# Two layers of graph attention in fp32: all groups' layer 0 before layer 1, and each projection as seven products of quarters in place of eight

## The chip, the cores and the metric

One core of a Trainium2 chip. The time is the device time of one execution in microseconds (us), the median of several executions.

## The reference, cut to what matters

`x` is 128 graphs of 128 nodes with 512 features, in fp32. Both layers have 8 heads of 64.

```python
# layer 0
Q, K, V = x @ W_q + b_q, x @ W_k + b_k, x @ W_v + b_v          # 512 x 512 each
scores = Q K^T / sqrt(64) + (x @ w_g[:D])[:, :, None] + (x @ w_g[D:])[:, None, :] + b_g + log(adj + 1e-9)
x = x + softmax(scores) @ V
# layer 1
q, k, v = x @ Wq.T + bq, x @ Wk.T + bk, x @ Wv.T + bv
logits = q k^T / sqrt(64) + log(clip(adj, 1e-8))
x = layer_norm(x + (softmax(logits) @ v) @ Wo.T + bo) * gamma + beta
```

Per group of four graphs these are three projections in layer 0 and four in layer 1, each a product of 512 x 512 (nodes by features) with 512 x 512 (weights). The softmax is computed without its maximum, and the log of the adjacency as a factor after `exp`.

## The kernel before

A group goes through layer 0 and, a step later, layer 1. The result of layer 0 stays in SBUF. A projection is 16 matmuls of 512 columns (V of layer 0: 32 of 256), each bank evicted by one instruction.

```python
def qk(W, bias, dst, e):
    p = ps.tile([P, G * N], F32, tag="proj", name=f"pqk_{g}_{L}_{e}")
    for c in range(KC):
        nc.tensor.matmul(p, W[L][:, c, e * P : (e + 1) * P], XT[g, L][:, :, c], start=(c == 0), stop=(c == KC - 1))
    nc.scalar.activation(dst[g, L][:, e].rearrange("p b n -> p (b n)"), p, AF.Identity, bias=bias[L][:, e : e + 1])
# ... cut: V, gate (two more columns of V's matmul in layer 0), scores, exp, multiply, second product
def part3(b):                                   # output projection, one graph
    aT = aTs[b // 2][:, b % 2]
    po = ps.tile([P, D], F32, tag="proj", name=f"po_{g}_{b}")
    for c in range(KC):
        nc.tensor.matmul(po, aT[:, c], WO[:, c], start=(c == 0), stop=(c == KC - 1))
    h = work.tile([P, D], F32, tag="h", name=f"h_{g}_{b}", bufs=3)
    nc.vector.tensor_tensor(h, po, X1[g][:, b], ALU.add)
    layer_norm(nc, small, h, GA, BE, minus_half, f"{g}_{b}")
# ... cut
for s in range(NG + 2):                         # one layer's projections beside another's attention
    a = proj_units(s, 0) if s < NG else []
    b = attn_units(s - 2, 1) if s >= 2 else []
    turned(merged(a, b), feature_units(s - 1, 1) if 1 <= s <= NG else [], 14)
    # ... cut
    a = proj_units(s - 1, 1) if 1 <= s <= NG else []
    b = attn_units(s, 0) if s < NG else []
    turned(merged(a, b), turn_units(s + 1) if s + 1 < NG else [], 14)
```

## Time and profile before

| | before |
|---|---|
| time, first three runs | 3999.66 us median (3997.59 to 4001.03) |
| span of the profiled run, mean granted TensorE clock | 3994.5 us, 0.992 |
| busy: TensorE, VectorE, GpSimd, ScalarE | 98%, 34%, 20%, 16% |
| HBM read, written | 84.16 MB, 33.55 MB |

The prediction below shows the lines. One more is used later: the granted clock in 40 equal slices of the span, in tenths of full speed (9 is 90% or more).

```profile
PEclk9999999999999999999999999999999999999988
```

It is at 90% or more until the last two slices.

### The profile page before, as it was taken

The page shows a single profiled execution, that of the slowest core. Times are in us where ns is not written, and L with a number is a line of the kernel's source. Part 1 is how long each engine was busy: PE and PEld are TensorE (multiplying, and loading weights), DVE is VectorE, ACT ScalarE, POOL GpSimd, SP SyncE. Part 2 cuts the span into 40 slices and gives each one's busy share as a digit, 9 for nine tenths or more (in the row PEclk, how much of TensorE's full clock was granted, in tenths as well). Part 3 has the DMA queues.
Part 4 walks back from the last instruction along what each step waited for, and adds up shares of the span by engine and source line. Part 5 has one row for each costly group of instructions (what it writes and reads, how often), then busy time and mean ns, then how long its engine had stood idle before and what let it go on. Part 6 is the DMA issues. An engine that isn't in the chain of part 4 may idle for free.

```text
span 3994.5 us, 41932 instructions
## 1 busy us (share of the span) xinstructions
PE 3902.6 (98%) x16386; PEld 2248.2 (56%) x16386; DVE 1376.7 (34%) x2723; ACT 636.5 (16%) x801; POOL 798.0 (20%) x839
## 2 busy tenths in 40 slices
PE   7999999999999999999999999999999999999986
PEld 4555555555555555555555555555555555555543
DVE  2233333333333333333333333333333333333332
ACT  1111111111111111111111111111111111111110
POOL 0122112122112122121221121221212211212221
PEclk9999999999999999999999999999999999999988
DMA  5212222222122122222221221222221222222111
GB/s 142 48 35 56 43 45 48 48 41 55 38 48 48 35 56 46 42 48 49 39 56 38 47 48 35 55 47 43 48 49 37 56 41 44 48 42 49 32 29 25
DMA packets 930039, 187.69 MB, mean 47 GB/s; under 512 B 892848, under 2 KB 892848, under 8 KB 929840
## 3 DMA queue, kind: packets, MB, share of 16 engines
q1 hardware_dynamic: 929840, 184.98, 22.5%
q8 instruction: 133, 2.18, 0.2%
q14 instruction: 66, 0.54, 0.0%
HBM read 84.16 MB, written 33.55 MB: 29 GB/s over the span
## 4 chain that ended last, share of the span: by engine, by line
PE 97%; SPq 1%; DVE 1%; issue 1%; POOL 0%; DMA 0%; ACT 0%; DVEq 0%; POOLq 0%
PE pqk L155 45%; PE av L249 12%; PE po L302 11%; PE pv L171 11%; PE pv L188 11%; PE s L224 7%; SPq L114 0%; SPq L86 0%; DVE t L239 0%; DMA wq<-in_L_gnn_W_q_dram 0%; POOL h L356 0%; POOL h L357 0%; DMA out_dram<-h 0%; DVE at L275 0%; DMA aT<-at 0%
## 5 line engine op out<-in xcount | busy, mean ns | idle before, releaser
L155 PE MATMUL pqk<-xT,wq 128*128 128x512 f32 x2048 | 942.5, 603 | 24.1 <-DMA wq<-in_L_gnn_W_q_dram 22.2
L155 PE MATMUL pqk<-xT,wk 128*128 128x512 f32 x2048 | 933.5, 598 | 0.0
L155 PEld LDWEIGHTS pqk<-xT,wk 128*128 128x128 f32 x2048 | 376.9, 190 | 428.1 <-issue 417.1
L155 PEld LDWEIGHTS pqk<-xT,wq 128*128 128x128 f32 x2048 | 373.1, 191 | 427.2 <-issue 410.4
L249 PEld LDWEIGHTS av<-v,t 128*128 128x128 f32 x4096 | 498.5, 194 | 130.9 <-issue 124.4
L239 DVE TENSOR_TENSOR t<-t,adjT 128x1024 f32<-128x1024 f32 x256 | 337.1, 1317 | 615.6 <-ACT t L232 615.6
L249 PE MATMUL av<-v,t 128*128 128x65 f32 x4096 | 498.3, 275 | 26.4 <-DVE at L275 24.0
L302 PE MATMUL po<-wo,aT 128*128 128x512 f32 x1024 | 466.0, 604 | 24.8 <-PE pv L171 14.0
L171 PE MATMUL pv<-wv,xT 128*128 128x256 f32 (+1 forms) x2048 | 465.3, 380 | 0.0
L188 PE MATMUL pv<-wv,xT 128*128 128x512 f32 x1024 | 453.1, 595 | 0.0
L171 PEld LDWEIGHTS pv<-wv,xT 128*128 128x128 f32 x2048 | 385.4, 189 | 93.3 <-issue 44.0
L282 POOL TENSOR_TENSOR x<-x,x 128x512 f32<-128x512 f32 x128 | 163.1, 1274 | 1096.2 <-DVE x L275 1096.2
L224 PEld LDWEIGHTS s<-qT,kT 64*128 64x128 f32 x4096 | 249.3, 188 | 191.0 <-issue 186.5
L302 PEld LDWEIGHTS po<-wo,aT 128*128 128x128 f32 x1024 | 194.9, 193 | 246.5 <-issue 205.5
L162 ACT ACTIVATE qT<-pqk,bq 128x512 f32<-128x512 f32 x256 | 175.9, 687 | 888.5 <-PE pqk L155 888.5
L188 PEld LDWEIGHTS pv<-wv,xT 128*128 128x128 f32 x1024 | 189.8, 190 | 215.2 <-issue 215.2
L162 ACT ACTIVATE kT<-pqk,bk 128x512 f32<-128x512 f32 x256 | 176.0, 688 | 798.4 <-PE pqk L155 798.4
L224 PE MATMUL s<-qT,kT 64*128 64x128 f32 x4096 | 298.4, 285 | 3.5 <-ACT t L232 3.5
L203 POOL TENSOR_TENSOR x<-x,bo 128x512 f32<-128x512 f32 x128 | 172.2, 1378 | 538.2 <-DMA xT<-x 538.2
L268 DVE TENSOR_SCALAR gated<-av,gate 128x8 f32<-128x8 f32 x128 | 28.9, 226 | 669.9 <-PE av L249 669.9
L232 ACT ACTIVATE t<-s 128x1024 f32<-128x1024 f32 x128 | 131.1, 1024 | 604.2 <-PE s L224 601.6
L176 DVE TENSOR_TENSOR v<-pv,bv 128x256 f32<-128x256 f32 x256 | 107.2, 419 | 299.4 <-PE pv L171 294.1
(39 smaller groups left out, 1578.9 us busy)
## 6 DMA issues: line engine op xcount, KB each, us to landing
x<-in_x_dram SPq DMA_DIRECT2D x32, 1024.0 KB, 5.5
xT<-in_x_dram SPq DMA_DIRECT2D x512, 64.0 KB, 2.5
xT<-x SPq DMA_DIRECT2D x512, 64.0 KB, 2.1
aT<-at SPq DMA_DIRECT2D x1024, 32.0 KB, 1.9
out_dram<-h SPq DMA_DIRECT2D x128, 256.0 KB, 2.1
adjT<-in_adj_dram SPq DMA_DIRECT2D x128, 64.0 KB, 2.3
wq<-in_L_gnn_W_q_dram SPq DMA_DIRECT2D x1, 1024.0 KB, 5.8
wk<-in_L_gnn_W_k_dram SPq DMA_DIRECT2D x1, 1024.0 KB, 8.0
```

The lines of the kernel that those rows point to most:

```text
L155: nc.tensor.matmul(p, W[L][:, c, e * P : (e + 1) * P], XT[g, L][:, :, c], start=(c == 0), stop=(c == KC - 1),)
L162: nc.scalar.activation(dst[g, L][:, e].rearrange("p b n -> p (b n)"), p, AF.Identity, bias=bias[L][:, e : e + 1])
L171: nc.tensor.matmul(p[:, 0:n], XT[g, L][:, b, c], wv0[:, c, s * W2 : s * W2 + n], start=(c == 0), stop=(c == KC - 1),)
L176: nc.vector.tensor_tensor(V[g, L][:, b, h2, 0:HD], p[:, 0:W2].rearrange("p (h d) -> p h d", d=HD), BV[L][:, s * W2 : (s + 1) * W2].rearran ...
L188: nc.tensor.matmul(p, XT[g, L][:, b, c], wv1[:, c], start=(c == 0), stop=(c == KC - 1))
L203: nc.gpsimd.tensor_tensor(X1[g][:, b], X1[g][:, b], BO, ALU.add)
L224: nc.tensor.matmul(s[:, r, c], KT[g, L][r * HD : (r + 1) * HD, c, b], QT[g, L][r * HD : (r + 1) * HD, c, b], start=True, stop=True,)
L232: nc.scalar.activation(t, s.rearrange("p r c j -> p (r c) j"), AF.Exp, scale=SCALE, **({"bias": AC[g][:, b, 1:2]} if L == 0 else {}),)
L239: nc.vector.tensor_tensor(t, t, AT2[g][:, L, b : b + 1, :].to_broadcast([P, H, N]), ALU.mult)
L249: nc.tensor.matmul(a4[:, h // KC, h % KC], t[:, (h % 2) * KC + h // 2], V[g, L][:, b, h], start=True, stop=True,)
L282: nc.gpsimd.tensor_tensor(dst, dst, X[g][:, b], ALU.add)
L302: nc.tensor.matmul(po, aT[:, c], WO[:, c], start=(c == 0), stop=(c == KC - 1))
```

## The change

Its intent is to take an eighth off the projections. The 512 x 512 operands are cut into quarters, and seven products of sums of quarters (Strassen's scheme in Winograd's form) replace the eight products. The sums of the weights are made once, which needs one layer's weights at a time in SBUF: hence layer 0 of all 32 groups first, its result to DRAM, then layer 1. The sums of X are made by GpSimd for each group. The seven products are combined by VectorE as they leave PSUM. The gate's two columns go from TensorE to VectorE, and layer 0's `b_v` is added to X for the residual by GpSimd.

```diff
+    ORDER = ("P1", "P6", "P7", "P5", "P2", "P3", "P4")
+    OPERANDS = {
+        "P1": (A11, "B11"), "P2": (A12, "B21"), "P3": (S4, "B22"), "P4": (NA22, "T4"),
+        "P5": (S1, "T1"), "P6": (S2, "T2"), "P7": (S3, "T3"),
+    }
...
+    SUMS = {"T1": ("B12", "B11"), "T2": ("B22", "T1"), "T3": ("B22", "B12"), "T4": ("T2", "B21")}
+    def sums(Bs, name, tag, which=tuple(SUMS)):
+        for s in which:
+            a, b = SUMS[s]
+            Bs[s] = act.tile([P, 2, 2, N], F32, tag=f"{tag}{s}", name=f"{s}_{name}")
+            nc.gpsimd.tensor_tensor(Bs[s], Bs[a], Bs[b], ALU.subtract)
+    def natural_units(t):
...
+            for s in range(2):                                   # the gate, in layer 0
+                junk = work.tile([P, D], F32, tag="junk", name=f"junk_{t}_{b}_{s}", bufs=1)
+                nc.vector.scalar_tensor_tensor(
+                    junk, XN[t, b // 2][:, b % 2], 1.0, WG[:, s], op0=ALU.mult, op1=ALU.mult,
+                    accum_out=C[t][:, s, b : b + 1],
+                )
+        def bias(k):
+            r = ROWS[L].rearrange("p (o d) -> p o d", o=1).to_broadcast([P, 2, D])
+            nc.gpsimd.tensor_tensor(XN[t, k], XN[t, k], r, ALU.add)
...
+        def unit(i):                                             # one product and its addition
+            if i in ("P1", "P6", "P7", "P5", "P4"):
+                t[i] = ps.tile([P, 2, D2], F32, tag="proj", name=f"p{name}_{i}", bufs=4)
+            bank = t[{"P2": "P1", "P3": "P5"}.get(i, i)]         # P2 onto P1's bank, P3 onto P5's
+            product(i, W, Bs, bank, side)
...
+            elif i == "P5":
+                o = dst(1, 1)
+                add(o, shape(bank, o), shape(t["u3b"], o))
...
+    for t in range(LAST + 1):                                    # 32 steps of layer 0, 32 of layer 1, one more
...
+        for i in range(max(len(proj), len(heads))):
+            if i < len(heads):
+                heads[i]()                                       # attention of the step before
+            if i < len(proj):
+                proj[i]()                                        # V, Q, K: 7 products each
...
+            if i >= 7 and side:
+                side.pop(0)()
+            for _ in range(2):
+                if has_out and proj and i >= 16 and turns:
+                    turns.pop(0)()                               # transposes of the attention output, then its sums
+            if i == 17 and sums_:
+                sums_.pop(0)()                                   # GpSimd's sums of the next group's X
+        for u in side + sums_:
+            u()
+        if has_out:
...
+            units, late = out_units()                            # output projection; late is layer norm
```

## The prediction

> **What bounds the kernel now.** I read the page first, then the chain of waits, then the groups by shape, then the timeline at the first group and at the end, where attention runs without projections beside it.
>
> ```profile
> PE 3902.6 (98%) x16386; PEld 2248.2 (56%) x16386; DVE 1376.7 (34%) x2723; ACT 636.5 (16%) x801; POOL 798.0 (20%) x839
> PE 97%; SPq 1%; DVE 1%; issue 1%; POOL 0%; DMA 0%; ACT 0%; DVEq 0%; POOLq 0%
> PE pqk L155 45%; PE av L249 12%; PE po L302 11%; PE pv L171 11%; PE pv L188 11%; PE s L224 7%; SPq L114 0%; SPq L86 0%; DVE t L239 0%; DMA wq<-in_L_gnn_W_q_dram 0%; POOL h L356 0%; POOL h L357 0%; DMA out_dram<-h 0%; DVE at L275 0%; DMA aT<-at 0%
> ```
>
> TensorE is the bound: 97% of the chain, 78% of it projections (45+11+11+11). The other engines are at most a third busy. The chain in order of time gives the pace of each kind:
>
> ```profile
> 1995.67 6.92 PE pv L188 x16
> 2002.59 1.73 PE av L249 x16
> 2011.24 1.09 PE s L224 x16
> 2061.59 3.47 PE pv L171 x16
> ```
>
> The profile has two records for each fp32 matmul. A record of 512 columns takes 6.92/16 = 0.4325 us, one of 256 takes 3.47/16 = 0.217, one of attention's second product (av) 1.73/16 = 0.108, one of the scores (s) 1.09/16 = 0.068. From these rows the work is 6144 x 0.4325 + 2048 x 0.217 + 4096 x 0.108 + 4096 x 0.068 = 2657 + 444 + 443 + 279 = 3823 us of 3994.5. The remainder is about 24 us at the start, about 46 at the end, and 2 to 3 us in each of 32 groups, mostly the 0.14 us by which a projection block after attention is longer.
>
> **What the Trainium skill says.**
> - TensorE: Matmul & The Clock Gate, Back-to-back issue gap: 256 columns take N/2.4 + 2.5 = 109 ns. Our records of 256 take twice that, and there are two of each matmul; I use the measured 0.217.
> - The same page, opening table: the queue pulls weight loads ahead of matmuls, and the other engines' queues are strict FIFO. So a matmul that waits holds all behind it. The trace agrees: at 3937.72 TensorE sat 0.99 us behind one PSUM read.
> - SBUF — State Buffer, Who interferes with whom: a VectorE instruction with two SBUF inputs and a GpSimd instruction that reads SBUF exclude one another. The trace agrees: a GpSimd add of 1.27 us took 2.17 beside such a multiply:
>
> ```profile
> 74.63 1.21 DVE L239 TENSOR_TENSOR t<-t,adjT 128x1024 f32<-128x1024 f32 x1
> 74.79 2.17 POOL L282 TENSOR_TENSOR x<-x,x 128x512 f32<-128x512 f32 x1 [73.38 <-DVE x L275]
> ```
>
> **The change part by part.**
>
> *TensorE work.* A projection of a group becomes 7 products of 4 matmuls of 256 columns. 7 projections x 32 groups x 28 = 6272 matmuls (the instruction order counts 6272), 12544 records x 0.217 = 2717 us, in place of 3101. That is **-384**, an eighth less (also the gate's two columns leave TensorE). One product is 1.73 us. New work: 2717 + 443 + 279 = 3439.
>
> *Work beside it.* VectorE: 1120 additions of 0.69 us with one PSUM input (773 us), 256 gate sums (about 180), a second adjacency transpose, less about 300 of old evictions and copies: some 2050 us. GpSimd: 384 operand sums of 1.27 (488), 128 wide bias additions (about 330), 96 residual additions (122), layer norm and residuals as before, less 172: about 1570 us. ScalarE about 760. None is near 3600 us as a sum; what counts is where each stands in its queue.
>
> *Layer 0 step* (one group's 21 products, the eight attention blocks of the previous group set between them). The instruction order shows good spacing. Two waits stay: the scores follow directly the last K product, whose addition takes 0.7 us after it (four of eight matmuls go first: about 0.5 us), and before it VectorE's gate sums, excluded by GpSimd at times, make K's sixth product late (about 0.5). Step: 21 x 1.73 + 4 x 1.09 + 4 x 1.73 + 8 x 0.14 + 1 = **50 us**. 32 steps.
>
> *Layer 1 step* (28 products). Here the instruction order puts scores 0 to 3 and av 0, 1 and half of 2 together, with only two output products in between at their start. Scores and av have now one buffer each and nothing runs beside. The end of the old kernel shows what that costs:
>
> ```profile
> 3930.03 1.16 PE L224 MATMUL s<-qT,kT 64*128 64x128 f32 x16
> 3932.32 1.16 PE L224 MATMUL s<-qT,kT 64*128 64x128 f32 x16 [1.12 <-ACT t L232]
> 3933.67 1.97 PE L249 MATMUL av<-v,t 128*128 128x65 f32 x16 [0.19 <-DVE t L239]
> 3937.72 1.97 PE L249 MATMUL av<-v,t 128*128 128x65 f32 x16 [0.99 <-DVE at L275]
> 3940.81 1.97 PE L249 MATMUL av<-v,t 128*128 128x65 f32 x16
> ```
>
> From the end of scores 0 (3931.12) to the start of av 2 are 9.7 us for 6.7 us of work: 3.0 us of wait. Then:
> 1. VectorE has two transposes of 0.65 before the read that frees av: +0.6.
> 2. After half of av 2 stands output product P6, which needs the third of GpSimd's sums; these start after the transposes, and 3 x 1.27 = 3.8 us later TensorE has waited 1.9.
> 3. The output's P3 overwrites a bank that is read only after u3 (VectorE), then two GpSimd additions of 1.27, then VectorE: 6.4 us from the end of P7 (about 18.2 to 24.1 on my clock, against 22.6): 1.5.
> 4. Layer norm's VectorE instructions stand in front of V's additions, and its GpSimd power and scaling stand between them: V's P3 is late by 1.3, and av 3 by 2.2 (VectorE stands until the fourth power, behind five 1.27 us instructions).
> Together 10.5 us. Step: 28 x 1.73 + 11.3 + 6 x 0.14 + 10.5 = **71 us**, 31 steps. A pair of steps is thus 121 us, as a group takes now (121.8, from the scores at 1957.74 to those at 2079.53).
>
> *Ends.* Start: X's blocks without the natural X ahead of them, but operand sums before P6: 26 us. The end: attention alone, moves over DMA (9.68 us of wait in the old end), sums, 7 products, layer norm: about 62 us beyond its matmuls, against 46. Loading and combining layer 1's weights on VectorE in place: 10. The round trip over DRAM is a group order of 32 steps apart and hidden: DMA is 22.5% busy now and moves perhaps a third more.
>
> *Sum.* Work 3439 + switches (8 x 32 + 6 x 31) x 0.14 = 62 + start 26 + layer 0 waits 32 + layer 1 waits 10.5 x 31 = 325 + weights 10 + end 62 = 3956, and some 4 us between span and time: **3960 us**, 1% faster. The expected gain of 384 goes mostly to waits that TensorE did not have.
>
> **The rivals.**
> *A: the waits are absorbed.* If layer 1 waits only 3 us a step, TensorE stays the bound at 3439 + about 290: some 3730 us, 7% faster. For it: every other engine is under 60% by sums, and an elaborate placing of the side work speaks of tuning. Against it: the order of each queue is fixed, and the cluster of scores and av is in it in every layer 1 step; the old trace shows its 3 us.
> *B: VectorE and GpSimd exclude one another much more.* GpSimd's work doubles, its sums and wide additions fall on gate sums (two SBUF inputs) and on the multiplies. With 2 us more in each step, 3960 + 64 x 2 = 4090: 2% slower. For it: 2.17 for 1.27 above, and 1483 ns mean for the layer norm's multiply. Against it: most of VectorE's new additions have one input in PSUM, and layer 0 has slack between its heads.
> *C: DMA becomes late* (blocks of X in layer 1 from DRAM in 128-byte pieces, behind output stores in one queue). The blocks are asked for at the end of K and needed some 20 us later; the old kernel issues 16 in 12 us. I give it little.
>
> **Range and chances.** The work term is firm to 10 us. The layer 1 wait is the loose one: 10.5 give or take 3.5 us, times 31, is 110 us either way; layer 0 give or take 1 us is 32; the ends 20. A change of this kind is more often kept when it gains, so I stretch a little more downward: 3840 to 4070. The 2% lines lie at 3920 and 4080. Faster 0.28, same 0.66, slower 0.06.
>
> **What would show it.** Right: 12544 projection records at 0.217; TensorE's busy time near 3500 rather than 3900, with 350 us or more idle, released by GpSimd's T sums, VectorE's e, av reads and the output's P3; idle of some 10 us in a step of the second half and 1 in the first; the half of the span at which layer 1 begins near 1670 us. Wrong: a second half with steps near 62 us (A); steps of layer 0 above 52 with long GpSimd and VectorE instructions (B); TensorE or VectorE waiting for blocks of X (C); a record of 256 columns well off 0.217, or a lower granted clock from the many short idles.

## More of the kernel before

The source gives an order of instructions, but a scheduler decides each engine's queue when the kernel is built, from its own estimates. The order that an engine executes is therefore read from the trace.

## The result, and the profile after

| | before | after |
|---|---|---|
| time, four runs each | 3998.62 us (3994.6 to 4001.03) | 4088.53 us (4087.49 to 4094.3) |
| span, mean granted clock | 3994.5 us, 0.992 | 4087.8 us, 0.957 |
| HBM read, written | 84.16, 33.55 MB | 159.92, 67.11 MB |

The ratio is 1.0229, 95% interval 1.0211 to 1.0247: 2.3% slower. A ratio here is the mean time of one kernel's fast runs over that of the other's of the same rounds, so not quite the ratio of the medians. The time lies above the predicted range.

The page of the changed kernel, busy times, clock in 40 slices and chain by engine:

```profile
PE 3705.2 (91%) x20754; PEld 3183.1 (78%) x20754; DVE 2245.3 (55%) x3827; ACT 705.9 (17%) x1217; POOL 1564.5 (38%) x1317
...
PEclk9999999999999999999999999999999989899986
...
PE 61%; DVE 14%; POOL 12%; SPq 6%; issue 5%; DMA 2%; ACT 0%; DVEq 0%; POOLq 0%; ACTq 0%
```

TensorE left the bound: 61% of the chain in place of 97%, VectorE and GpSimd together 26%. Its busy time fell by 197 us only, where its work fell by 384, and the clock drops below 0.9 in some slices of the second half: part of the difference is matmuls that ran slowly. The clock record in the trace, which the page averages as PEclk, has 50 stretches at half speed, 353 us together; the kernel before has 6, 67 us.

From the view of waits (engine, tile and line, what released it: us in total, times, longest):

```profile
PE pk_P L203 <- DVE kT L220: 78.7, 30, 2.7
...
PE po_P L203 <- POOL T_o L163: 70.1, 30, 7.6
...
PE av L336 <- DVE o L356: 55.7, 48, 4.0
...
PE po_P L203 <- DVE h L220: 46.6, 32, 1.5
PE pv_P L203 <- DVE v L220: 46.2, 26, 8.9
```

The first is a wait of layer 0, 2.6 us in nearly every step; the others are of layer 1. In the timeline (start, us, engine, line, what, count, idle before), layer 0 at the end of K:

```profile
1000.26 2.36 POOL L186 TENSOR_TENSOR xn<-xn,bv 128x1024 f32<-128x1024 f32 x1 [12.11 <-DVE junk L175]
...
1000.76 2.41 DVE L175 SCALAR_TENSOR_TENSOR junk<-xn,wg 128x512 f32<-128x512 f32 x1
...
1003.21 1.64 DVE L175 SCALAR_TENSOR_TENSOR junk<-xn,wg 128x512 f32<-128x512 f32 x1
...
1005.38 1.14 DVE L175 SCALAR_TENSOR_TENSOR junk<-xn,wg 128x512 f32<-128x512 f32 x1
...
1007.18 0.69 DVE L220 TENSOR_TENSOR kT<-pk_P,u3k 128x512 f32<-128x512 f32 x1
...
1007.92 2.42 PE L203 MATMUL pk_P<-xT,wk 128*128 128x256 f32 x8 [2.71 <-DVE kT L220]
...
1010.14 3.20 PE L203 MATMUL pk_P<-T,wk 128*128 128x256 f32 x8
```

A gate sum (`junk`) takes about 0.7 us undisturbed. The first here takes 2.41 beside GpSimd's wide bias addition, the next two are long beside GpSimd's sums. They stand in VectorE's queue ahead of the addition of K's P5, whose bank P3 overwrites, so TensorE stands 2.71 us. Then it is slow: the two products of eight records take 2.22 us (1007.92 to 1010.14) and 3.12 (to the next start at 1013.26), where a product takes 1.73. The clock record has half speed from 1009.36 to 1012.77. This slow stretch came in about half of the steps: they last 51.94 or 53.62 us.

Layer 1, the waits in one step:

```profile
3010.65 1.99 PE L203 MATMUL pv_P<-wv,xT 128*128 128x256 f32 x8 [1.44 <-DVE v L220]
...
3016.99 1.97 PE L336 MATMUL av<-v,e 128*128 128x65 f32 x16 [1.72 <-DVE o L356]
...
3050.16 1.16 PE L316 MATMUL s<-qT,kT 64*128 64x128 f32 x16 [1.11 <-ACT e L324]
...
3055.51 1.97 PE L336 MATMUL av<-v,e 128*128 128x65 f32 x16 [0.99 <-DVE o L356]
...
3059.02 1.08 PE L336 MATMUL av<-v,e 128*128 128x65 f32 x8 [0.45 <-DVE o L356]
3062.88 8.00 PE L203 MATMUL po_P<-wo,T_o 128*128 128x256 f32 x28 [2.78 <-POOL T_o L163]
...
3072.36 1.99 PE L203 MATMUL po_P<-wo,aT 128*128 128x256 f32 x8 [1.48 <-DVE h L220]
```

These add up to 9.97 us. Behind the wait for `T_o`, 28 records take 8.00 us, where 28 x 0.216 = 6.05: slow again, by 2 us. The step, from V's first product at 3000.42 to the next at 3075.05, is 74.6 us: 28 x 1.73 + 4 x 1.09 + 4 x 1.73 = 59.7 of work, 10.0 of waits, 2.0 of slow records, and 2.9 that is left for changes between blocks and for restarts after the seven waits. I had counted six changes at 0.14, 0.84. The same remainder in a step of norm_later (below), with as many changes but one wait, is 1.3, so most of the 2.9 seems to come with the waits; no run took it apart.

Where the time is, from the starts of the steps in the timeline, against the terms of the prediction:

| part | predicted | measured |
|---|---|---|
| up to the second step | 26 + 21 x 1.73 = 62 | 61 |
| 32 steps of layer 0 | 32 x 50 = 1600 | 1690, 52.8 each |
| 31 steps of layer 1 | 31 x 71 = 2201 | 2262, 73.0 each |
| the rest | 95 | 75 |

So layer 0 is 90 us over, layer 1 61 us, the rest 20 under. Layer 1's steps are not alike: 64 to 66 us for the first three, 72 to 79 for the next seventeen, 71.7 to 71.9 for the last ten. The instruction order goes with it: TensorE's queue starts close to the source's order and drifts from step to step into the cluster of scores and av. Nor is the step above typical in its waits: over the 31 steps TensorE's waits add up to 227 us, 7.3 a step, and the last ten wait 5.3 us each and spend 10.2 us each at half clock.

### The profile page after: what moved, and what is told of

Read it like the earlier page. It is cut to its first block, busy times and chain, and to the rows that moved or that the text cites. A ratio compares the mean times of both kernels' runs of the same rounds, so it can differ in the third digit from the quotient of the medians.

```text
span 4087.8 us, 54690 instructions
## 1 busy us (share of the span) xinstructions
PE 3705.2 (91%) x20754; PEld 3183.1 (78%) x20754; DVE 2245.3 (55%) x3827; ACT 705.9 (17%) x1217; POOL 1564.5 (38%) x1317
## 3 DMA queue, kind: packets, MB, share of 16 engines
HBM read 159.92 MB, written 67.11 MB: 56 GB/s over the span
## 4 chain that ended last, share of the span: by engine, by line
PE 61%; DVE 14%; POOL 12%; SPq 6%; issue 5%; DMA 2%; ACT 0%; DVEq 0%; POOLq 0%; ACTq 0%
PE pq_P L203 17%; PE pv_P L203 13%; PE pk_P L203 12%; PE av L336 8%; PE po_P L203 7%; DVE junk L175 5%; SPq L123 5%; PE s L316 4%; POOL T_o L163 3%; POOL h L542 2%; POOL h L543 2%; POOL rs L540 1%; DVE kT L220 1%; POOL u3co L409 1%; POOL u3do L409 1%
## 5 line engine op out<-in xcount | busy, mean ns | idle before, releaser
L336 PEld LDWEIGHTS av<-v,e 128*128 128x128 f32 x4096 | 519.4, 201 | 88.3 <-issue 36.0
L336 PE MATMUL av<-v,e 128*128 128x65 f32 x4096 | 523.5, 283 | 59.2 <-DVE o L356 55.7
L203 PE MATMUL pv_P<-wv,T 128*128 128x256 f32 x2048 | 490.2, 387 | 3.0 <-POOL T L163 3.0
L203 PE MATMUL pk_P<-T,wk 128*128 128x256 f32 x2048 | 476.3, 386 | 0.0
L203 PE MATMUL pq_P<-T,wq 128*128 128x256 f32 x2048 | 463.6, 379 | 0.0
L203 PEld LDWEIGHTS pk_P<-T,wk 128*128 128x128 f32 x2048 | 400.0, 195 | 58.3
L203 PE MATMUL pk_P<-xT,wk 128*128 128x256 f32 x1536 | 371.6, 389 | 78.7 <-DVE kT L220 78.7
L203 PE MATMUL pv_P<-wv,xT 128*128 128x256 f32 x1536 | 384.8, 394 | 62.9 <-DVE v L220 46.2
L203 PEld LDWEIGHTS pq_P<-T,wq 128*128 128x128 f32 x2048 | 389.7, 190 | 53.2
L203 PEld LDWEIGHTS pv_P<-wv,T 128*128 128x128 f32 x2048 | 378.9, 191 | 58.0 <-POOL T L163 4.0
```

Of the source, the lines that this page charges most:

```text
L203: nc.tensor.matmul(dst, lhsT, rhs, start=(i in ("P1", "P6", "P7", "P5", "P4") and o == 0 and k == 0), stop=(k == 1), skip_group_check=True,)
L336: nc.tensor.matmul(a4[:, h // KC, h % KC], e[:, (h % 2) * KC + h // 2], V[t][:, b, h], start=True, stop=True)
```

## The experiments

My theory after this: TensorE stands behind places in the other queues, and what looks like a lower clock follows from the standing. The rivals: the time of VectorE or GpSimd is used up whatever the order; the lower clock comes from loading weights more densely; the split into layers itself costs.

### pe_order: TensorE's queue held in the source's order

```diff
+    mm = lambda *a, **k: tc.keep_in_program_order(nc.tensor.matmul(*a, **k))
...
-                nc.tensor.matmul(
+                mm(
```

(at all four places of the fast path)

> The changed kernel with one thing more: every matmul keeps its place in the order in which the source writes it (scores and av of a group set between the seven-product units in both layers). Theory 1 (in layer 1 the order of TensorE's queue, which the scheduler lets drift so that scores and av stand together and the output products behind half of av 2, costs the time): steps of layer 1 go from 72 to 75 us to 64 to 66, as the first three of them (64.9, 63.9, 65.9 us, where the order has not drifted yet) already are; 30 steps x 7.5 = 225 less: about 3860 us. Layer 0 stays at 51.9 to 53.6. Rival 1 (the lower granted clock, 0.957 for 0.992, is itself the cause, from the denser weight loads): the time stays near 4090 and the clock near 0.957. Rival 2 (VectorE and GpSimd are simply too loaded in layer 1): steps stay above 70 us.

Measured: 3971.74 us (3966.36 to 3977.45), ratio to before 0.9928 (0.9911 to 0.9944); 117 us less than the changed kernel. The cluster's waits are gone, layer 0 is as it was (51.8 and 53.5 us), layer 1's steps are 68.3 us. The order was worth half of what I expected (3860 us). The rest of the gain turned into another wait, which order_nobias0 shows below.

### nobias0: layer 0 without the wide bias additions

The result stays right, as `b_v` is zero in this case.

```diff
-        return u + [lambda k=k: bias(k) for k in range(2)]
+        return u + ([] if L == 0 else [lambda k=k: bias(k) for k in range(2)])
```

> The changed kernel without GpSimd's two wide additions of b_v to the natural X in each step of layer 0 (b_v is zero in the data, so the result stays right; for other data it would be wrong). Theory 1 (in K's phase VectorE's gate sums, with two inputs in SBUF, and GpSimd's wide addition exclude one another: a gate sum takes 2.4 us for 0.69, K's sixth product waits 2.7 us, and then runs at half clock in some steps): K's wait falls below 0.7 us, gate sums from a mean of 1073 ns to below 850, steps of layer 0 from a mean of 52.7 to about 49.7, 31 x 3 = 93 less: about 3995 us. Rival (VectorE's own load in that phase, without GpSimd, makes K late): wait 2 us or more, and the time within 1% of 4089.

Measured: 4013.86 us (4011.65 to 4016.47), ratio 1.0038 (1.0021 to 1.0055); 75 us less than the changed kernel. I had expected 3995. Layer 0's steps are 50.2 us, all alike, and gate sums fall from a mean of 1073 to 849 ns; K's wait fell to 1.03 us, not below 0.7. Layer 1 is unchanged. So most of layer 0's excess came with this addition beside the gate sums.

### order_nobias0: both

> Both edits together. Theory 1: the two causes are in different layers, so they add: 4089 - 225 - 93 = about 3770 us, 6% below the kernel before. Rival 1 (clock): no better than the better of the two alone by more than 20 us.

Measured: 3902.49 us (3901.07 to 3907.3), ratio 0.9763 (0.9746 to 0.9779). The gains add up: 117 + 75 = 192 against 186. But 3902 is far from 3770, and the clock is still 0.964. TensorE and GpSimd at the end of K in layer 1:

```profile
3046.77 7.86 PE L94 MATMUL po_P<-wo,T_o 128*128 128x256 f32 x24 [4.05 <-POOL T_o L164]
```

```profile
3041.14 1.27 POOL L164 TENSOR_TENSOR T<-T,xT 128x512 f32<-128x512 f32 x1 [2.63 <-PE pk_P L94]
3043.01 2.48 POOL L164 TENSOR_TENSOR T_o<-aT 128x512 f32<-128x512 f32 x2 [0.60 <-DVE aT L383]
3045.45 1.26 POOL L164 TENSOR_TENSOR T_o<-aT,T_o 128x512 f32<-128x512 f32 x1
```

GpSimd waits for K's last product to make X's fourth sum, and two transposes of the attention output stand on VectorE behind K's last addition. Only then come the output's sums. TensorE stands 4.05 us, and its next 24 records take 7.7 us to the start of the following one, where they take 5.2.

### eight: the new structure with eight products

Layers split and the result of layer 0 over DRAM as in the changed kernel, TensorE in the source's order, but quarters multiplied as they are: no sums, and each bank evicted once.

```diff
+        return [lambda m=m, n=n, k2=k2: unit(m, n, k2) for m in range(2) for n in range(2) for k2 in range(2)]
...
-            nc.gpsimd.tensor_tensor(Bs[s], Bs[a], Bs[b], ALU.subtract)
```

> The changed kernel's structure (layer 0 of all groups, result to DRAM, then layer 1; matmuls of 256 columns, source order on TensorE) with eight products of quarters in place of seven: no operand sums, no combined weights, evictions as simple as in the kernel before. It tells the two halves of the change apart. Theory 1 (splitting the layers and the way over DRAM cost nothing to speak of; what the seven products save on TensorE is an eighth of the projections): layer 0 step 24 x 1.73 + 11.3 + 1.3 = about 54.5, layer 1 step 32 x 1.73 + 11.3 + 1.5 + some 2 = about 70, a pair 124.5 for 121.8 before: about 4060 us (4000 to 4110), and 200 to 280 us slower than order_nobias0. Rival (the split itself, with its loads from DRAM, loses the time): above 4150 us, with waits for blocks of X or natural X.

Measured: 4029.69 us (4029.35 to 4030.7), ratio 1.0078 (1.0061 to 1.0095), clock 0.993. Steps are 54.4 and 68.7 us, close to their TensorE work. So the split, the matmuls of 256 columns and the trip over DRAM cost 0.8% together: DMA is not the cause. Against order_nobias0 of the same rounds it is 127 us slower, where I expected 200 to 280: the waits there still ate part of the saving.

### sums_early: the output's sums ahead of X's fourth sum

On order_nobias0: sums, additions and the attention output's transposes are held in the source's order, and the source places transposes and sums earlier.

```diff
+            keep(nc.gpsimd.tensor_tensor(Bs[s], Bs[a], Bs[b], ALU.subtract))
+            add = lambda o, i0, i1: keep(nc.vector.tensor_tensor(o, i0, i1, ALU.add))
+            keep(nc.vector.transpose(v, v))
...
+    TURNS = {14: 2, 18: 2, 19: 1}
-            for _ in range(2):
-                if has_out and proj and i >= 16 and turns:
+            if has_out and proj and i in TURNS:
+                for _ in range(TURNS[i]):
                     turns.pop(0)()
```

> On top of order_nobias0 (TensorE's queue in the source's order, layer 0's wide additions dropped: 3902): the attention output's four transposes on VectorE and its four GpSimd sums come before X's fourth sum and before K's last addition. Theory (the order of the queues makes the waits, and each wait of some 3 us brings a stretch of slow products with it): the output projection's wait of 4.05 us on T_o falls below 1 us and its slow records with it, 24 records in about 5.2 us again; a layer 1 step goes from about 69 to 62.5 us, some 6.5 x 31 = 200 us less: about 3700 (3670 to 3760), the granted clock in layer 1 back from 0.96 towards 0.985. Rival (a lower clock is granted in layer 1 because seven products load weights more densely, whatever the waits): the clock stays near 0.96, the wait alone goes (4 x 31 = 125 us) or comes back elsewhere: 3780 or more.

Measured: 3747.11 us (3744.54 to 3752.47), ratio 0.9375 (0.936 to 0.9391), clock 0.988. The wait and the slow records behind it are gone:

```profile
2539.11 5.34 PE L95 MATMUL po_P<-wo,T_o 128*128 128x256 f32 x24
...
2547.00 1.99 PE L95 MATMUL po_P<-wo,aT 128*128 128x256 f32 x8 [0.81 <-DVE h L222]
...
2570.30 3.45 PE L95 MATMUL pv_P<-wv,xT 128*128 128x256 f32 x8 [1.65 <-DVE v L222]
```

The clock came back although weights are loaded more densely now (busy 83% of the span against 78% in the changed kernel): that rival falls. The time is 47 us above my 3700, because of the last line. VectorE stands in V behind layer norm, TensorE waits 1.65 us there, and in 5 of the last 28 steps the product after it runs at half speed (3.25 us to the next start). Steps are 64.25 or 65.9 us, not 62.5.

### bias_late: the bias addition kept, but elsewhere

On sums_early, with layer 0's additions done one step later, after heads 0 and 3, away from the gate sums. This is right for any bias again.

```diff
+        if L == 0:
+            LATE[t] = [lambda k=k: bias(k) for k in range(2)]
+            return u
...
+            if i in (0, 3) and LATE.get(t - 1):
+                LATE[t - 1].pop(0)()
```

> As sums_early, but layer 0's wide bias additions are kept (right for any bias) and done one step later on GpSimd, after heads 0 and 3, away from VectorE's gate sums. Theory (not the 240 us of GpSimd work, but its place beside the gate sums made layer 0's step 2.5 us longer): within 20 us of sums_early, so about 3710, layer 0's steps 50.2 to 50.8 us and gate sums near 0.7 us each. Rival (GpSimd's amount of work slows VectorE wherever it stands): layer 0's steps near 52 again, some 60 to 75 us slower than sums_early.

Measured: 3751.85 us (3748.07 to 3756.05), ratio 0.9386 (0.937 to 0.9401), 5 us above sums_early. Gate sums and the bias addition in the groups by shape (busy us, mean ns; idle before), first of the changed kernel, then of this one:

```profile
L175 DVE SCALAR_TENSOR_TENSOR junk<-xn,wg 128x512 f32<-128x512 f32 x256 | 274.8, 1073 | 5.4
...
L186 POOL TENSOR_TENSOR xn<-xn,bv 128x1024 f32<-128x1024 f32 x64 | 155.0, 2423 | 416.3 <-DVE junk L175 377.8 <-issue 38.4
```

```profile
L178 DVE SCALAR_TENSOR_TENSOR junk<-xn,wg 128x512 f32<-128x512 f32 x256 | 180.9, 707 | 6.7 <-DMA wg<-in_L_gnn_w_g_dram 1.3
...
L189 POOL TENSOR_TENSOR xn<-xn,bv 128x1024 f32<-128x1024 f32 x64 | 151.5, 2368 | 0.0
```

GpSimd does the same work, and the gate sums are undisturbed. The adjacency multiply pays for it now (mean 1481 ns against 1240 in sums_early), but it stands where nobody waits for it: layer 0's steps are 49.1 us in both. The amount of GpSimd's work was not the matter, its place was. One limit: no run kept the addition in its old place with the queues held as they are here.

### fill_wait: useless matmuls in the wait

To test whether the standing makes the slow records: order_nobias0, with eight matmuls into the idle scores banks right after the output's first product.

```diff
+            units[0]()
+            if t < LAST:
+                fill = ps.tile([P, 2, KC, N], F32, tag="s", name=f"fill_{t}")
+                f2 = fill.rearrange("p r c j -> p r (c j)")
+                for k in range(FILL):
+                    mm(f2[:, 0, 0:D2], WO[1][:, 0, 0, 0:P], WO[1][:, 0, 0], start=True, stop=True)
+            for u in units[1:]:
```

> order_nobias0 (3902) with useless work added: after the output projection's first product TensorE does eight matmuls of 256 columns on resident weights into the idle scores banks, whose result nobody reads, 16 records x 0.216 = 3.46 us inside its wait of 4.05 us for T_o. The result stays right. Theory (a stretch of idleness of some 3 us or more is what puts the next 28 to 32 records at half clock): the wait shrinks to about 0.6 us, the 24 records after it take 5.2 us again in place of 7.5, a step of 68.3 becomes 65.9: 2.36 x 31 = 73 us less, about 3830 (3815 to 3850), with the granted clock in layer 1 up from 0.95 to about 0.99. Rival (the slow records come from something else, power or density of weight loads, or are an artefact of the records): the time stays at 3902 or grows.

Measured: 3954.79 us (3953.05 to 3956.69), ratio 0.9892 (0.9876 to 0.9909): 52 us slower than order_nobias0, so a miss. It is inconclusive. The scheduler had moved VectorE's and GpSimd's queues: the output's sums now came before they were needed, so the filler filled nothing, and other waits came (1.66 us in V, in two steps 5.5; up to 2.44 us for av in a dozen steps). I repeated it with the queues held (hold and hold_fill).

### norm_later: layer norm out of V's way

On bias_late: the statistics and the power of all four blocks right at the start of the next step, the scaling after V.

```diff
             for _ in range(2):
+                if i < 2 and early:
+                    early.pop(0)()                # bn_stats, bn_aggr, power, all held in order
...
-        side += late + (natural_units(t) if t < LAST else [])
+        side = late + side + (natural_units(t) if t < LAST else [])   # scaling, gamma, beta from i = 7 on
```

> bias_late (3752) with layer norm cut in two: its sums and power of all four blocks at the start of the next step, its scaling after V, so that VectorE no longer stands in V behind a GpSimd power that is behind three additions. Theory: TensorE's wait of 1.67 us for V's P3 and of 0.54 before av 2 go, and with them the half-speed product that follows the former in one step of three; a layer 1 step falls from a mean of 64.75 to 62.5 us (28 x 1.73 + 11.3 + 0.84 = 60.6 of work, 0.8 before the output's P3, the rest switches): 2.2 x 31 = 70 us, about 3685 (3665 to 3715). Rival: VectorE's or GpSimd's time is used up there and the wait appears elsewhere (Q's second product, T_o): within 1% of 3752.

Measured: 3651.34 us (3648.05 to 3654.8), ratio 0.9132 (0.9117 to 0.9147), with a correct result. It is below my range (3665 to 3715) and beats both kernels: 8.7% faster than before. Layer 1's steps are 61.7 us throughout, where TensorE's work is 60.6. The page:

```profile
PE 3540.8 (97%) x20754; PEld 3078.7 (84%) x20754; DVE 2115.2 (58%) x3827; ACT 708.7 (19%) x1217; POOL 1529.0 (42%) x1317
...
PEclk9999999999999999999999999999999999999997
```

The same count of TensorE's instructions as in the changed kernel has 164 us less busy time, and the slices of lower clock are gone. Against eight (4029.69, other rounds, on another chip whose before was 3999.11 against 3998.93) the seven products save 378 us; 7 products a pair of steps, 32 pairs, 1.73 us each are 387. Once the queues are in order, nearly the whole eighth arrives.

### hold and hold_fill: the wait put back, and filled

hold is norm_later with the output's sums made late on purpose; hold_fill has the filler of fill_wait in that wait.

```diff
-    TURNS = {14: 2, 18: 2, 19: 1}
+    TURNS = {16: 2, 20: 3}
...
+            keep(nc.vector.transpose(v, v))       # X's blocks
+            keep(nc.vector.transpose(a, a))       # the adjacency's
```

> norm_later (3651) with the long wait put back on purpose, and nothing else: two of the attention output's transposes and all its GpSimd sums go after K's last product, all VectorE transposes held in the source's order too. TensorE should wait some 4 us for T_o again, as in order_nobias0. Theory (such a wait costs itself and then a stretch of half-speed products): the 24 records behind it take 7.5 us in place of 5.2, a step goes from 61.7 to about 68.1 us, 31 x 6.4 = 198 us, about 3850 (3825 to 3875), granted clock in layer 1 0.95 to 0.96. Rival (the slow records are not caused by the wait): 61.7 + 4.05, 3777, clock near 0.99.

> hold with the same useless eight matmuls in the wait as fill_wait had; by the instruction order the queues of VectorE, GpSimd and ScalarE are now the same as hold's, instruction by instruction (in fill_wait they were not). Theory: the wait shrinks to about 0.6 us, the records behind it run at full speed, a step is 61.7 + 4.05 = 65.8 us: about 3777, so some 70 us (55 to 85) faster than hold though TensorE does 31 x 3.46 = 107 us more work; granted clock about 0.99. Rival (the slow records have another cause): the same as hold within 10 us, or slower.

Measured: hold 3767.93 us (3767.0 to 3768.66), ratio 0.9424 (0.9408 to 0.9439); hold_fill 3744.43 us (3743.37 to 3747.34), ratio 0.9367 (0.9351 to 0.9382). The output's P6, P7 and P5 (24 records) in steps of hold:

```profile
2689.39 6.94 PE L95 MATMUL po_P<-wo,T_o 128*128 128x256 f32 x24 [3.08 <-POOL T_o L166]
...
2755.64 5.45 PE L95 MATMUL po_P<-wo,T_o 128*128 128x256 f32 x24 [2.95 <-POOL T_o L166]
...
2885.71 7.13 PE L95 MATMUL po_P<-wo,T_o 128*128 128x256 f32 x24 [2.95 <-POOL T_o L166]
```

and in a step of hold_fill:

```profile
2610.82 3.62 PE L95 MATMUL fill<-wo 128*128 128x256 f32 x16
2614.27 5.34 PE L95 MATMUL po_P<-wo,T_o 128*128 128x256 f32 x24
```

The wait was 2.95 us here, not 4, so both times are below what I expected, and the gap between them is 23 us, not 55 to 85. By its time alone, hold would even fit the rival (3777); the slow records decide. The pair is clean, as VectorE, GpSimd and ScalarE execute the same instructions in the same order in both traces. In hold, 13 of the 30 steps are slow behind the wait, 66.3 to 66.5 us in place of 65.04. In hold_fill none is: all are 65.0 to 65.2. TensorE does 31 x 3.46 = 107 us more of useless work, and the kernel is 23 us faster.

The clock record shows the same. In hold most of the wait falls into one stretch of 3.41 us, and the next stretch is granted half speed (stretch, its length; busy us of PE, PEld, DVE, ACT, POOL; PEclk, DMA, GB/s):

```profile
2685.62:2689.03 3.41, 0.69 (x4) 0.27 (x2) 1.03 (x2) 0.59 (x1) 2.22 (x2) 1.00 0.65 102
2689.03:2692.44 3.41, 3.05 (x7) 2.51 (x8) 0.00 (x0) 0.00 (x0) 3.41 (x4) 0.50 0.63 100
2692.44:2695.86 3.42, 3.42 (x17) 2.98 (x17) 1.39 (x2) 0.00 (x0) 2.28 (x3) 1.00 0.41 63
```

After the first 130 us and before the last 100, hold has 13 such stretches, one in each slow step; hold_fill and norm_later have none. The standing is what makes the slow records: the clock is halved after it.

## Why the prediction was wrong, point by point

- **The work of TensorE** was right. 12544 projection records at 0.216 us each, seven products in place of eight, as norm_later against eight confirms.
- **The order of layer 1** was right, and its waits were right in kind: 10.5 us were listed, and the step above shows 9.97, nearly one by one. Their sum was not: 10.5 x 31 = 325 us were forecast, and 227 were measured. That the layer still came out 61 us over is because the terms below cost more than the waits saved, so its near agreement (71 against 73.0) is partly luck. pe_order undid the cluster, and half of the expected gain turned into the next wait in the same queue.
- **The layer 0 step is where it failed**, in the term "VectorE's gate sums, excluded by GpSimd at times, make K's sixth product late (about 0.5)". It was mis-sized: the wait was 2.71 us. I had put all 256 gate sums at 180 us, 0.7 each; they took 1.07, because GpSimd's bias addition and sums fall exactly on them. The other 0.5, for the scores behind K's last product, did not come. nobias0 takes the addition away and finds 50.2 us, the predicted step; bias_late keeps it in another place and loses 5 us of 3747.
- **A term was missing.** I named a lower clock from the short idles as something that could go wrong, but put nothing in the sum. The products behind a wait of 2 to 4 us can cost some 2 us more: the alternation of 51.94 and 53.62 in layer 0, and about 2 us in a step of layer 1. hold and hold_fill show the cause. Layer 1's changes between blocks and restarts after waits, 2.9 us in place of 0.84 in the step above, are a second, mis-sized term. Work and waits apart, layer 1 took 186 us where 26 were forecast (2262 - 31 x 59.65 of work - 227 of waits, against 31 x 0.84).
- **The ends** were put 20 us too high. No run took them apart.
- **The rivals.** B gave 4090 and named exclusion as its reason. That is right for layer 0, where the gain of nobias0 is 75 us of the 90; in layer 1 the excess is the slow records and the changes and restarts, so B came to nearly the right sum with the wrong parts. A, the absorbed waits, is what the same instructions do once they are placed otherwise: 3651. C did not happen: eight shows the trip over DRAM to cost under 1%, together with all else that it changes.

What stays open: why the order in the steps of layer 1 drifts as it does. In the 72 to 79 us steps the waits are 7 to 10 us and the time at half clock 3.4 to 10.2 us; I took one step apart, and not the longest.

## What to carry to other kernels

When the bound engine is given less work and the others more, do the sum for the queues, not for the engines: for each instruction that the bound engine waits for, look at what stands ahead of it in its own queue and what runs beside it on an engine that excludes it. In these kernels a wait of 2 us or more in front of TensorE could halve its clock for the next 3.41 us or more, at a cost of up to some 2 us; from about 3.2 us on it nearly always did. A large saving that does not arrive is worth looking for in the order before the change is given up.

## What the Trainium skill lacked or had wrong

- TensorE: Matmul & The Clock Gate, section "What's actually happening", says that the clock is halved after at least one idle window of about 3.4 us, and that the windows run freely. The clock records of all twelve traces agree on the windows: the clock changes between full and half only on a grid of 3.413 us. But the window need not be idle. I took the windows at full clock in which TensorE's only work was projections, without the first 60 and last 90 us, and counted each record as busy for 0.216 us from its start (0.432 for 512 columns). The next window was at half clock in all 114 cases with less than 35% busy, in 16 of 23 with 35 to 40%, and in none of 6189 with more; with attention's records in the window the split is less sharp. As an estimate from these counts, some 2.1 us of standing within one window (60 to 65% of it) is enough, and where the wait falls on the grid decides: the same wait of about 3 us was followed by slow records in 13 of 30 steps of hold. The page has short idles that throttle, in the section "A second HAM failure mode: psum-queue depth-cycling", but gives no lengths. Counted by length in eight kernels of seven products (those without the filler), for waits of over 0.5 us with no other wait in the 5 us before, the block behind was slow by over 0.8 us in 2 of 387 cases below 1.2 us, 32 of 151 for 1.2 to 2.2, 34 of 104 for 2.2 to 3.2, and 61 of 64 for 3.2 to 4.5.
- The same page has no case of useless work that pays. Here 3.46 us of unused matmuls in a wait of 2.95 us made every step 65.0 us, where 13 of 30 had been 66.3 or more.
- SBUF — State Buffer, section "Who interferes with whom", has the exclusion right: a gate sum of 0.71 us took 2.41 beside a GpSimd addition of 2.36. It says nothing of the queue: the addition behind the gate sums has one input in PSUM, does not contend by that section, and came so late all the same that TensorE waited 2.71 us.
